# One table part of three loads split into DMAs of 123, 3 and 2 rows

## The chip, the cores and the metric

The kernel runs on one core of one Trainium2 chip. The metric is the device time of one launch in microseconds (us), the median of three runs. A profile of one further execution is read beside it.

## The reference

For 1024 sequences of 50 item numbers the kernel looks up embeddings of 128 values, takes running means over time, normalises them over the batch, runs a spiking neuron over the 50 steps, and multiplies the mean spike count of each sequence with the whole embedding table:

```
e = emb_table[r_seq]                       # 1024 x 50 x 128, row 0 of the table counts as zero
uF = cumsum(e, axis=1) / minimum(t, length)
y = (uF - mean) * rsqrt(var + eps) * gamma + beta
v, spike = scan over the 50 steps          # v += (y - v) / 2; spike when v >= 1; v -= spike
scores = spikes.mean(over steps) @ emb_table.T     # 1024 x 100001, float32
```

The scores are 410 MB, and writing them is most of the traffic.

## The kernel before

The first stage gathers the 50 steps' embeddings by indirect DMA on GpSimd and runs the 50 steps. Beside it SP loads the first 40 parts of the table. A part is 1024 table rows (`HALF`), kept as 128 partitions of 8 table rows each, 4 KB a partition; 98 parts make the table, and the last one has only 673 rows.

The second stage makes the scores. It goes through 21 columns of the output, of 2, 3 and then 6 parts (`WIDTHS`; the last 13 columns have 6), and in each through eight blocks of 128 sequences. A block of a 6-part column is 24 matmuls (`product`, L160, each part being a high and a low half and two banks), six evictions out of PSUM, in turn on DVE (L502) and ACT (L504), and one store of 3 MB on SP's queue (`store`, L169). There are three output buffers of that size, so at most three stores are in flight, and an eviction into a buffer waits until the store before it has landed.

A part is made ready for the matmuls by `prepare`: eight transposes on TensorE (`turned`, L136), a copy on ACT (L152) and a subtraction on DVE (L153). `ready()` calls it between the blocks, about one column ahead of its use, in the order of the parts.

The table parts from 40 on are loaded in the second stage by `fetch`, three parts at a time (1.5 MB), in blocks 1 and 4 of a column:

```
            if n in (1, 4) and c >= MIDDLE and to_fetch < parts:
...
                    fetch(r, k, to_fetch, GROUP // 2)
                    to_fetch += GROUP // 2
```

These loads go out on ACT's queue (`engine = nc.sync if q < held else nc.scalar`), each as one DMA of 128 partitions by three parts (L109). The last load is different, since the last part is short: it goes as one row of 512 B (L120) and 84 rows of 4 KB (L125). The buffers are groups of six parts; two groups are used in turn.

The instructions of each engine run in the order in which the program gives them. The waits between engines, and the semaphores that DMAs complete on, are put in by the framework.

Of the kernel before, what the change touches and what calls it, by code (L numbers as in the profile page):

```python
# [20 lines left out]
P = 128  # L21
BN_EPS = 1e-5
V_TH = 1.0
HALF = 1024
KQ = HALF // P
# [8 lines left out]

WIDTHS = 4 * [2] + 4 * [3] + 13 * [6]
NARROW, MIDDLE = 4, 8


@with_exitstack
def rec_kernel(  # L40
# [49 lines left out]
    def size(q):  # L90
        return min(HALF, N - q * HALF)
# [4 lines left out]
    def group(g):  # L96
        at = g if g < AHEAD else AHEAD - 2 + g % 2
        r = rowp.tile([P, GROUP, HALF], F32, tag=f"rows{at}", name=f"rows_{g}")
        for k in range(GROUP):
            rows[g * GROUP + SHIFT + k if g else k + ASIDE * (k >= TWICE)] = r[:, k, :]  # L100
        return r

    def fetch(r, k, q, n):

        engine = nc.sync if q < held else nc.scalar
        n = min(n, parts - q)
        whole = n - (size(q + n - 1) < HALF)
        if whole:
            engine.dma_start(  # L109
                out=r[:, k : k + whole, :],  # L110
                in_=table[q * HALF : (q + whole) * HALF, :].rearrange("(q p k) d -> p q (k d)", p=P, k=KQ),
            )
        if whole < n:
            full, rest = divmod(size(parts - 1), KQ)
            c1 = (parts - 1) * HALF
            r = r[:, k + whole, :]
            if rest:
                at = full - full % 32
                nc.vector.memset(r[at : at + 32, :], 0.0)
                engine.dma_start(  # L120
                    out=r[full : full + 1, : rest * D],
                    in_=table[c1 + full * KQ : N, :].rearrange("(o k) d -> o (k d)", o=1),
                )
            if full:
                engine.dma_start(  # L125
                    out=r[:full, :],
                    in_=table[c1 : c1 + full * KQ, :].rearrange("(p k) d -> p (k d)", k=KQ),
                )
# [43 lines left out]
    with ExitStack() as ph:  # L172
# [16 lines left out]
        nc.sync.dma_start(out=gb[:, 1:2], in_=beta.rearrange("(d o) -> d o", o=1))  # L189
        first = group(0)  # L190
        fetch(first, 0, 0, TWICE)
        spare = asidep.tile([P, ASIDE, HALF], F32, tag="aside", name="spare")
        for k in range(ASIDE):
            rows[TWICE + k] = spare[:, k, :]
        fetch(spare, 0, TWICE, ASIDE)
        fetch(first, TWICE, SHIFT, GROUP - TWICE)
        for g in range(1, AHEAD):
            fetch(group(g), 0, g * GROUP + SHIFT, GROUP)
# [91 lines left out]
        def over(t, v):  # L290

            d = lp.tile([P, B], BF16, tag="d", name=f"d_{t}")
            nc.scalar.activation(d, v, AF.Identity, bias=less)  # L293
            return d
# [7 lines left out]
        whole = slice(0, B)  # L302
# [6 lines left out]
        for t in range(T):  # L309
# [30 lines left out]
            r = sp.tile([P, 1], F32, tag="r", name=f"r_{t}")  # L340
# [14 lines left out]
            q = sp.tile([P, 1], F32, tag="q", name=f"q_{t}")  # L355
# [20 lines left out]
            if not last:  # L376
# [6 lines left out]
                d = over(t, v)  # L383
# [3 lines left out]
                if t in (T - 8, T - 6):  # L387
                    q = (t - T + 8) // 2
                    pair(q)
                    prepare(q, vp.tile([P, HALF], F32, tag="v1", name=f"pt_{q}"))  # L390
                    if q == TWICE - 1:
                        for k in range(TWICE):
                            rows[GROUP + ASIDE + k] = first[:, k, :]
                        nc.sync.dma_start(
                            out=first[:, :TWICE, :],
                            in_=table[(GROUP + ASIDE) * HALF : (GROUP + SHIFT) * HALF, :].rearrange(
                                "(q p k) d -> p q (k d)", p=P, k=KQ
                            ),
# [55 lines left out]
    for c, W in enumerate(WIDTHS):  # L454
# [34 lines left out]
        for n in range(NB):  # L489
# [26 lines left out]
            if n in (1, 4) and c >= MIDDLE and to_fetch < parts:  # L516
                g, k = divmod(to_fetch - SHIFT, GROUP)
                if k or to_split >= (g - 1) * GROUP + SHIFT:
                    if k == 0:
                        r = group(g)  # L520
# [23 lines left out]
```

## Time and profile before

| | |
|---|---|
| median of three runs | 1576.82 us (1576.77 to 1577.33) |
| the profiled execution | 1636.12 us, span 1633.9 us |
| first store of the second stage | 574.0 us |
| PE, DVE, ACT busy | 66%, 58%, 41% of the span |
| SP's DMA queue (q1) | 430.86 MB, 62.7% of sixteen engines' span |
| ACT's DMA queue (q10) | 30.23 MB, 4.6% |
| HBM | 77.69 MB read, 409.60 MB written |

The profile lists groups of instructions by source line, engine and operation with their count, total and mean time, and what the engine waited for before them. A stage's table gives each engine's busy time in a stretch of the span and the share of time in which the sixteen DMA engines were busy. The chain of waits goes back from the last instruction to whatever released it. All times count from the span's start. Besides these views the trace holds a record for every DMA packet (start, duration, queue, size, but not the engine) and for every update of a semaphore.

### The profile page before, as it was taken

To read this page: it belongs to the slowest core of one execution; us is meant where nothing else is said; L and a number is where in the kernel's file an instruction comes from. 1 tells how busy PE (TensorE), PEld (TensorE's weight loads), DVE (VectorE), ACT (ScalarE), POOL (GpSimd) and SP (SyncE) were. 2 spreads that over 40 slices of the span, in tenths; PEclk is the share of its full clock that TensorE was granted. 3 is DMA by queue.
4 is the path that set the end of the run, shared out by engine and by line. 5 is a ranking of instruction groups with operands and counts; after the bars stand their busy time and mean duration, and the time that the engine had idled before them with its cause. 6 is when DMAs were issued, how large, how long until landed. Compare 5 with 4: busy or idle time off the path is not lost.

```text
span 1633.9 us, 12229 instructions
## 1 busy us (share of the span) xinstructions
PE 1085.1 (66%) x4452; PEld 804.9 (49%) x4452; DVE 944.4 (58%) x1125; ACT 667.5 (41%) x697; POOL 382.2 (23%) x406
## 2 busy tenths in 40 slices
PE   4333422342343498898988878888788888888884
PEld 2112211122122266676866666666666666666663
DVE  5666755676575865665755554555555555545552
ACT  2333322333333355455544444444444444444442
POOL 7666666776766500000000000000000000000000
PEclk9999999999999999999999999999999999999998
DMA  9611111111112189999999999999999999999997
GB/s 349 235 49 49 47 45 44 51 47 44 52 45 60 50 352 416 405 422 415 402 431 423 428 431 425 425 421 418 426 429 421 416 416 417 430 425 417 423 420 330
DMA packets 51313, 488.12 MB, mean 299 GB/s; under 512 B 10079, under 2 KB 10336, under 8 KB 30004
## 3 DMA queue, kind: packets, MB, share of 16 engines
q1 hardware_dynamic: 30752, 430.86, 62.7%
q0 software_dynamic: 12800, 26.24, 5.5%
q10 hardware_dynamic: 7700, 30.23, 4.6%
q8 instruction: 35, 0.57, 0.1%
q14 instruction: 26, 0.21, 0.0%
HBM read 77.69 MB, written 409.60 MB: 298 GB/s over the span
## 4 chain that ended last, share of the span: by engine, by line
DMA 49%; DVE 12%; PE 11%; another core or an unknown queue 8%; POOL 7%; ACT 6%; issue 5%; ACTq 0%; DVEq 0%; SPq 0%; POOLq 0%
DMA scores<-o 46%; PE po L160 10%; POOL e L207 7%; ACT o L504 5%; DVE uF L330 2%; DMA e<-in_L_rec_emb_table,idx 2%; DVE bs L331 2%; DVE v L374 2%; DVE negv L297 2%; DVE o L502 1%; DVE count L300 1%; PE pre L321 1%; ACT v L371 1%; PE pre L281 0%
## 5 line engine op out<-in xcount | busy, mean ns | idle before, releaser
L502 DVE TENSOR_SCALAR o<-po 128x1024 f32<-128x1024 f32 x391 | 463.7, 1221 | 345.8 <-DMA scores<-o 314.0
L504 ACT ACTIVATE o<-po 128x1024 f32<-128x1024 f32 (+1 forms) x391 | 388.9, 1018 | 540.9 <-DMA scores<-o 326.2
L207 POOL DMA_INDIRECT e<-in_L_rec_emb_table,idx x400 | 381.5, 954 | 179.7 <-issue 108.2
L160 PE MATMUL po<-pairs,countB 128*128 128x512 f32 (+1 forms) x1120 | 295.9, 410 | 67.6 <-ACT o L504 52.5
L160 PEld LDWEIGHTS po<-pairs,countB 128*128 128x128 f32 x1120 | 212.9, 195 | 131.3 <-ACT o L504 69.9
L281 PE MATMUL pre<-zT,ls 128*128 128x512 f32 x100 | 78.9, 791 | 270.0 <-DVE uF L330 226.9
L160 PE MATMUL po<-pairs,countC 128*128 128x512 f32 (+1 forms) x840 | 228.1, 418 | 43.6 <-ACT o L504 43.4
L160 PEld LDWEIGHTS po<-pairs,countC 128*128 128x128 f32 x840 | 162.7, 200 | 89.2 <-ACT o L504 55.2
L281 PEld LDWEIGHTS pre<-zT,ls 128*128 128x128 f32 x100 | 29.5, 296 | 309.0 <-DVE uF L330 256.3
L321 PE MATMUL pre<-ident,e 128*128 128x128 f32 x400 | 125.9, 436 | 79.4 <-DMA e<-in_L_rec_emb_table,idx 62.8
L330 DVE SCALAR_TENSOR_TENSOR uF<-rlen,pre 128x512 f32<-128x512 f32 x100 | 68.0, 680 | 166.9 <-remote 132.5
L321 PEld LDWEIGHTS pre<-ident,e 128*128 128x128 f32 x400 | 80.4, 209 | 126.1 <-DMA e<-in_L_rec_emb_table,idx 92.9
L153 DVE TENSOR_TENSOR pairs<-pt,pairs 128x1024 fp32r<-128x1024 f32 x70 | 84.6, 1217 | 90.1 <-ACT pairs L152 90.1
L341 ACT ACTIVATE r<-mv,eps 128x1 f32<-128x1 f32 x50 | 14.7, 295 | 281.7 <-DVE mv L337 185.9
L136 PE MATMUL pt<-ident,rows 128*128 128x128 f32 (+1 forms) x768 | 109.8, 290 | 9.9 <-issue 8.2
L136 PEld LDWEIGHTS pt<-ident,rows 128*128 128x128 f32 (+1 forms) x768 | 99.5, 153 | 27.9 <-issue 12.6
L160 PE MATMUL po<-hi,countB 128*128 128x512 f32 x208 | 86.1, 414 | 16.3 <-ACT o L504 11.1
L160 PE MATMUL po<-lo,countB 128*128 128x512 f32 x208 | 83.6, 402 | 0.0
L293 ACT ACTIVATE d<-v,less 128x1024 bf16<-128x1024 f32 x49 | 54.5, 1113 | 63.5 <-DVE v L374 37.6
L152 ACT CAST pairs<-pt 128x1024 fp32r<-128x1024 f32 x70 | 70.5, 1007 | 16.4 <-PE pt L136 16.3
L160 PE MATMUL po<-hi,countC 128*128 128x512 f32 x156 | 66.3, 425 | 15.2 <-ACT o L504 15.2
L160 PE MATMUL po<-pairs,countA 128*128 128x512 f32 x280 | 70.1, 395 | 9.5 <-ACT o L504 9.5
(85 smaller groups left out, 869.2 us busy)
## 6 DMA issues: line engine op xcount, KB each, us to landing
scores<-o SPq DMA_DIRECT2D x96, 3072.0 KB
scores<-o SPq DMA_DIRECT2D x32, 1536.0 KB
scores<-o SPq DMA_DIRECT2D x30, 1024.0 KB
rows<-in_L_rec_emb_table ACTq DMA_DIRECT2D x19, 1536.0 KB
scores<-o SPq DMA_DIRECT2D x8, 2896.5 KB
rows<-in_L_rec_emb_table SPq DMA_DIRECT2D x5, 3072.0 KB
e<-in_L_rec_emb_table,idx POOLq DMA_INDIRECT x400
rows<-in_L_rec_emb_table SPq DMA_DIRECT2D x2, 1024.0 KB
```

The source lines that it names most:

```text
L136: nc.tensor.transpose(pt[:, k0 : k0 + pw], r[:pw, k0 : k0 + D], ident[:pw, :pw])
L152: nc.scalar.copy(vh, vp)
L153: nc.vector.tensor_tensor(vl, vp, vh.bitcast(F32), ALU.subtract)
L160: nc.tensor.matmul(po[:, :kw], lhsT=counts[n], rhs=part[:, k0 : k0 + kw], start=j == 0, stop=j == 1,)
L207: nc.gpsimd.indirect_dma_start(out=es[t][:, n * P : (n + 1) * P], out_offset=None, in_=table, in_offset=bass.IndirectOffsetOnAxis(ap=idx[: ...
L281: nc.tensor.matmul(pre[h], lhsT=l, rhs=zT[:, h * BANK : (h + 1) * BANK], start=t == 0, stop=False, skip_group_check=True,)
L293: nc.scalar.activation(d, v, AF.Identity, bias=less)
L297: nc.vector.scalar_tensor_tensor(negv, d, 0.0, v, ALU.is_ge, ALU.subtract)
L321: nc.tensor.matmul(pre[h][:, k : k + P], lhsT=e[:, h * BANK + k : h * BANK + k + P], rhs=ident, start=False, stop=last, is_transpose=True, ...
L330: nc.vector.scalar_tensor_tensor(uF[:, cs], rlen[:, cs], 1.0 / (t + 1), pre[h], ALU.max, ALU.mult)
L502: nc.vector.tensor_scalar_mul(o[:, h0 : h0 + hw], po[:, :hw], 1.0 / T)
L504: nc.scalar.mul(o[:, h0 : h0 + hw], po[:, :hw], 1.0 / T)
```

## The change

For three of the loads, those whose first part is 43, 61 or 79, the third part (45, 63 and 81) is taken out of the DMA of three parts. It is loaded by three DMAs of 123, 3 and 2 partitions, issued one after the other on the same queue, and then the other two parts follow as one DMA of 128 partitions by two parts. All other loads, the data and the buffers are as before.

```
+LOW = (43, 61, 79)
...
         whole = n - (size(q + n - 1) < HALF)
+        if q in LOW:
+            whole -= 1
+            n = whole
+            one = r[:, k + whole, :]
+            src = table[(q + whole) * HALF : (q + whole + 1) * HALF, :].rearrange("(p k) d -> p (k d)", k=KQ)
+            p0 = 0
+            for pw in (123, 3, 2):
+                engine.dma_start(out=one[p0 : p0 + pw, :], in_=src[p0 : p0 + pw, :])
+                p0 += pw
+            assert p0 == P
         if whole:
             engine.dma_start(
                 out=r[:, k : k + whole, :],
```

## The prediction

> **What bounds the kernel now.** I read the stages first, then who waits for whom, then the chain of waits, and last the raw records of the stores' completions. The stretches of the second stage (columns: length, then busy time of PE, weight load, DVE, ACT, POOL, then granted clock, DMA share, GB/s):
>
> ```profile
> core 0: us, PE busy (x) PEld busy (x) DVE busy (x) ACT busy (x) POOL busy (x), PEclk, DMA share, GB/s
> 870.00:930.00 60.00, 47.44 (x213) 37.26 (x212) 31.76 (x28) 25.55 (x27) 0.00 (x0) 0.97 1.00 428
> 1240.00:1300.00 60.00, 49.71 (x216) 39.52 (x215) 32.29 (x28) 26.20 (x27) 0.00 (x0) 0.91 0.99 413
> ```
>
> DVE and ACT are about half idle, PE has a fifth free, and the sixteen DMA engines have none. The waits of 880 to 1470 us say the same: the evictions wait for a store to give its buffer back.
>
> ```profile
> DVE o L502 <- DMA scores<-o: 186.2, 66, 5.4
> ACT o L504 <- DMA scores<-o: 178.1, 64, 3.7
> ```
>
> In the chain of waits each store stands with some 20 us, because three are always in flight:
>
> ```profile
> 905.91 20.95 DMA scores<-o
> 926.86 0.02 issue
> ...
> 939.53 21.96 DMA scores<-o
> ```
>
> A store counts sixteen completions, one per DMA engine, and the trace records the time of each. For the store issued at 913.79 fifteen land between 929.8 and 931.9 and the sixteenth at 935.1. It is so for every store from 790 us on: one engine, call it the slow one, is 3 to 9 us behind the middle. The packet records show why. A packet starts 3 to 4 ns before its predecessor on the same engine ends, so one engine's packets can be followed: the slow one needs 936 ns on average for a store row of 24 KB, most others 912. It has no gap, and its stores end 7.5 us apart (8.8 while a load runs). So **the slow engine's own packets set the pace**, and the others are ahead until they run out of stores.
>
> **The skill.** The Trainium skill, "DMA: Bandwidth & Descriptors", section "Why a DMA increments its semaphore by 16 and not by 1", says that a DMA from SP or ACT runs on k engines, k the largest number up to 16 that divides the slowest dimension of both sides, on the lowest-numbered ones, the sequencer writing the rest of the count itself. The rows of the last table part bear on it (durations in ns, min/median/max):
>
> ```profile
> L109 ACTq DMA_DIRECT2D rows<-in_L_rec_emb_table x19: 374/375/469, 864.6 to 1469.8; - x19
> L120 ACTq DMA_DIRECT2D rows<-in_L_rec_emb_table x1: 487/487/487, 1512.4 to 1512.4; - x1
> L125 ACTq DMA_DIRECT2D rows<-in_L_rec_emb_table x1: 808/808/808, 1512.9 to 1512.9; - x1
> ```
>
> L109's loads of 128 rows land with sixteen completions. L125's of 84 rows shows fourteen, between 10.7 and 11.8 us, and one update at 1.0 us, the sequencer's; L120's single row shows one at 5.5 us. The rule holds here and the forecast goes by it: 123 = 3 x 41 and 3 rows run on engines 0 to 2, 2 rows on engines 0 and 1.
>
> The same page, section "Latency and other measured facts", says that engines 7 and 15 are usually the slow ones. The trace can't number the slow engine, but it excludes some: its chain contains packets of the 84-row load (five of six are found), so it is among the first fourteen; and L120's 512 B packet, which must be engine 0's, sits in a chain of 912 ns packets that completes the store of 1511.89 at 1523.7, where the slow one lands at 1531.5. I take engines 0 to 2 to be ordinary ones.
>
> **The change part by part.** It touches the loads issued at 904.87, 1107.27 and 1309.05 (first parts 43, 61, 79).
>
> *Removed.* Each of engines 3 to 15 has 16 load packets instead of 24. A 4 KB packet takes 159 ns less the 4 of overlap, so the slow engine is spared 8 x 0.155 = 1.24 us a load, 3.7 in three.
>
> *Added on engines 0 to 2.* 41 + 1 + 1 packets (engine 2 has no row of the last DMA) in place of 8: 35 x 0.155 = 5.4 us a load. These engines are ahead: by 5.0 us at the store issued at 913.79, in the middle of the sixteen, by 6.5 at 1117.35 and 6.4 at 1319.47. The lead grows by 0.23 us a store (936 less 912 ns, eight times, and a little more), so 24 stores between two such loads bring back 5.5.
>
> *Added on ACT.* Three more issues, each 0.4 to 0.8 us by the three rows above: at most 2.2 us, ahead of evictions for which ACT has 2.4 to 4 us of waiting at each store. Nothing; without that cover 2.2 a load.
>
> *Added waits.* SP's and ACT's DMAs take eight completion semaphores in turn, and one that takes a used semaphore waits for its owner first: ahead of the store at 948.61 SP's records have a wait on the semaphore of the load issued at 904.87. A load gets its semaphore two stores before its place in time. The changed load takes four. The first, of the 123 rows, then comes round at the store of 922.42, where the whole turn came round only at 948.61. So SP holds that store, and every one behind it, until 123 rows have landed. Load and store packets alternate on an engine, a pair taking 1.06 us; by the end of the store of 913.79 (930.0 on a middle engine) some 21 load packets are done, the store queue is empty, and the last 20 follow back to back: 930.0 + 20 x 0.155 = 933.1. The store is then issued at 933.2 and reaches the engines 0.84 later (stores on an idle engine land 8.6 us after issue, eight packets take 7.3 and the receipt 0.48): 934.05. The slow engine ends its packets of 913.79's store at 935.14 - 0.48 - 1.24 = 933.4. It idles 0.65 us.
>
> At the other two the lead starts from nothing, since the hold lets all engines begin together: 5.5 us after 24 stores. The hold ends 5.5 - 20 x 0.155 = 2.4 before the old landing, the store reaches the engines 1.5 before it, and the slow engine is free 1.72 before it: 0.2 us of idling each. Sum for ordinary engines 0 to 2: -3.7 + 0.65 + 0.2 + 0.2 = -2.65.
>
> *Instruction fetches.* 16 KB packets of the instruction queue come every 35 us, each on another engine, and put it 1.9 us behind: four of sixteen stood so at 930, five had been hit in each later stretch. If one of the three engines is among them, that load loses 1.9. With four or five of fifteen hit, it is more likely than not in any one load. I take it for one load of the three, since the hits seem to pass from engine to engine and engines 0 to 2 are neighbours: -2.65 + 1.9 = -0.75.
>
> *What is late next.* The two-part DMA comes behind in the ring of engines 0 to 2: 16 packets. Some 6 to 9 go while the store queue is empty, the rest alternate: landed at 947. It is wanted first at 950.94 by the transposes of part 43:
>
> ```profile
> 950.94 0.48 PEld L136 LDWEIGHTS pt<-ident,rows 128*128 128x128 f32 x3
> 951.17 0.38 PE L136 MATMUL pt<-ident,rows 128*128 128x128 f32 x2
> ```
>
> and by the store of 948.61, which has its semaphore. Hidden by 2 to 4 us. Parts 44 and 45 are wanted at 979.8 and 989.5.
>
> The operation that the trace doesn't show is a load on three engines, whose rows go to partitions that other engines serve. Its packet lies between 155 ns (the same size above) and 300 ns (the slowest hundredth of such packets): 0 to 20 x 0.145 = 2.9 us a load. I take 155, since loads at L125 with fourteen engines show nothing else, and keep 2.9 x 3 for the range. Below nothing the cost can't go further than 3.7 us, the packets taken off the slow engine.
>
> **The forecast.** The profiled execution took 1636.12 us, span 1633.9 and 2.2 around it; it becomes 1635.4. The runs' median is 59 us lower; [...]I carry the -0.75 over: 1576.1. A measurement tells some 0.2%, 3.2 us, from no change, so this is no change; its own range is 1574.2 (no load hit) to 1579.9 (all three hit).
>
> **Rivals.**
> 1. *No hold, late transposes (slower).* If the semaphores fall so that no store is held, the stores keep alternating with the loads. Then 59 load packets and seven stores from 904.5 on end at 904.5 + 7 x 7.27 + 59 x 0.155 = 964.6, landed at 965. PE stands at part 43's transposes from 951 on; four products (0.93 each), their evictions and the transposes bring the next store to 965 + 6.2 = 971.2, on the engines at 972. The slow engine is free at 967.1. Loss 4.9 - 1.24 = 3.7 a load, 11 in all: 1588. It decides once the two-part DMA lands over 2 us behind 960. For it: the ring's order. Against it: the wait seen at 948.61.
> 2. *The slow engine exists only under the profiler (slower).* Then engines 0 to 2 have no lead: the hold ends 3.1 behind the others' store, the next starts 0.94 later and the 0.48 of the receipt counts too; the relief is paid back within that: 4.5 us lost a load, 13.6 in all: 1590.4. For it: the profiled run is 59 us longer. Against it: the first stage has 127 us of stalls under "another core or an unknown queue" that can account for that.
> 3. *The slow engine is 1 or 2 (slower).* It pays 5.4 a load and the hold on top, 7 each: 1598. Against: two of thirteen numbers, and the page's 7.
> 4. *The full relief (faster).* No idling, -3.7: 1573.1. It needs the three engines further ahead than the middle.
>
> **How the numbers follow.** No change or nearly (first case) 0.40, of which 0.04 below -3.2; rival 4 another 0.18; rival 1 0.12; rival 2 0.18; rival 3 0.05; costlier packets or fetches 0.07. Faster by over 0.2%: 0.18 + 0.04 = 0.22. Within: 0.40 - 0.04 = 0.36. Slower: the rest, 0.42. The range 1572.9 to 1590.5 leaves out rival 3 and a third of rival 2 above, together 0.11, and 0.07 below. Cases of both signs hold most of the chance; the likeliest one's range stands above.
>
> **What would show it.** In the changed profile: the loads of 43, 61 and 79 as four issues each; 123 rows with three completions near 28 us after issue; SP waiting some 11 us ahead of the third store after them; the early completions of the next store bunched with the slow one's; the slow engine's stores 8 packets shorter over those loads. PE idle for over 10 us at part 43's transposes would show rival 1, a gap of 4 us or more on the slow engine rivals 2 or 3. A time over 1580 or under 1573 would say that the lead of engines 0 to 2 was misjudged.

## The result, and the profile after

The changed kernel takes 1578.95 us in the median of 14 runs (1577.70 to 1582.37), the kernel before 1576.81 us (1576.05 to 1577.59) beside it: 2.1 us more, ratio 1.0016, 95% interval 1.0009 to 1.0024. The forecast was 1576.1, 0.75 us less than before, in a range of 1574.2 to 1579.9. The result lies in that range, but where no change or a small gain was forecast it is a small loss, and its interval excludes no change. The six of the 14 runs with a mean granted TensorE clock of 0.81 took 1577.70 to 1578.63 us, the eight at 0.94 to 0.96 took 1578.94 to 1582.37.

The profiled run of the changed kernel (clock 0.955) is one of its longest, 1581.87 us with a span of 1579.7. Its first stage is 59 us shorter than in the profile of before (the first store goes out at 514.9 us instead of 574.0), so the spans can't be compared. I compare the second stage: the last 105 stores, from the landing of the first to that of the last. It took 848.00 us before and 853.05 after, **5.05 us more** in this pair of profiles. A time of before less some 60 us is the same place in the profile after.

The stretches that answer to those of the prediction (811 to 871 and 1180 to 1240 us), with three short ones around the first changed load:

```profile
core 0: us, PE busy (x) PEld busy (x) DVE busy (x) ACT busy (x) POOL busy (x), PEclk, DMA share, GB/s
811.00:871.00 60.00, 48.43 (x219) 37.54 (x218) 32.30 (x28) 26.00 (x28) 0.00 (x0) 0.97 1.01 430
860.00:868.00 8.00, 6.41 (x32) 5.00 (x31) 3.83 (x4) 2.96 (x4) 0.00 (x0) 1.00 1.00 424
869.00:878.00 9.00, 7.87 (x39) 6.25 (x38) 5.98 (x6) 4.40 (x5) 0.00 (x0) 1.00 0.90 285
880.00:890.00 10.00, 3.11 (x14) 2.21 (x12) 1.22 (x1) 0.52 (x1) 0.00 (x0) 0.91 0.97 412
1180.00:1240.00 60.00, 46.77 (x215) 36.81 (x214) 32.09 (x28) 25.83 (x27) 0.00 (x0) 0.97 1.01 428
```

Over the longer stretches the DMA engines are full, as before, and move 428 to 430 GB/s (428 and 413 before). Between 869 and 878 us they are still 0.90 busy, but they move 285 GB/s: here the stores stand still. The evictions' waits for stores between 821 and 1411 us are fewer and longer, since a held store holds up its buffer (longest 10.1 and 11.3 us; 5.4 and 3.7 before):

```profile
DVE o L513 <- DMA scores<-o: 189.1, 61, 10.1
ACT o L515 <- DMA scores<-o: 187.9, 60, 11.3
```

The chain of waits around the first changed load. Where the chain of before had a store at each step, it now has the load:

```profile
823.51 19.19 DMA scores<-o
...
846.04 32.04 DMA rows<-in_L_rec_emb_table
878.08 0.02 issue
878.10 0.03 SPq L180
...
878.59 20.76 DMA scores<-o
```

SP stands behind the 123 rows that ACT issued at 846.04 us, and issues three stores one after the other from 878.15 on. It does so at each of the three loads, 71.2 us in all, the longest 24.6 (total, times, longest in the waits of SP's DMA queue, which had no such line before):

```profile
SPq L180 <- DMA rows<-in_L_rec_emb_table: 71.2, 3, 24.6
```

The loads themselves, in the rows of the tile (L116 has the DMAs of 123, 3 and 2 rows, L120 the loads as before and the two-part DMAs, L131 and L136 the short last part):

```profile
L120 ACTq DMA_DIRECT2D rows<-in_L_rec_emb_table x19: 374/375/1186, 805.8 to 1418.2; - x19
L116 ACTq DMA_DIRECT2D rows<-in_L_rec_emb_table x9: 270/1053/1257, 846.0 to 1255.6; - x9
L131 ACTq DMA_DIRECT2D rows<-in_L_rec_emb_table x1: 253/253/253, 1460.1 to 1460.1; - x1
L136 ACTq DMA_DIRECT2D rows<-in_L_rec_emb_table x1: 1039/1039/1039, 1460.4 to 1460.4; - x1
```

The transposes of part 43, which need the two-part DMA, start at 897.77 with no wait noted behind them:

```profile
897.77 1.03 PEld L147 LDWEIGHTS pt<-ident,rows 128*128 128x128 f32 x8
898.00 1.04 PE L147 MATMUL pt<-ident,rows 128*128 128x128 f32 x8
```

The records of the completions, worked out from the trace (us after issue; the gap runs from the end of the last engine's packets of the store before the hold, its landing less 0.48, to the held store's arrival on the engines, its issue plus 0.84):

```
load of   123 rows, 3 completions   two-part DMA: 13 engines, other 3   next load: 13 engines, other 3   gap
43        31.4 31.6 32.0            20.8-21.4     31.6-32.2              7.3-8.4    24.2-27.5           4.2
61        32.3 32.4 34.0            20.3-22.3     32.5-33.9              7.4-7.7    18.5-27.0           5.3
79        31.1 31.8 33.7            20.1-22.9     31.8-33.6              6.7-7.4    14.9-26.7           5.3
```

And the held store of 878.15 itself lands 8.6 to 9.3 us after issue on thirteen engines, 12.4 to 12.5 on three. How late the changed kernel is at the same store (the landing of the whole store after minus before, in us, from the first of the 105 on):

```
store        19     20     23     33     43     44     48     58     67     68     72     82     92    104
after     -0.72  +6.10  +4.22  +1.37  +0.80  +8.70  +6.34  +4.74  +3.58 +11.44  +9.10  +7.58  +5.33  +5.05
                  held                         held                         held
```

Each hold throws the kernel back by 7 to 8 us, of which some 2 come back with the next load's packets, which the gap has already taken in; then it gains 0.1 to 0.3 us a store, and from store 94 on nothing more.

Who is last in between can be read from the sixteen completions of each store. The slow engine is told from the others by its pace: with no load under way it loses some 0.2 us a store on them. The same lateness (against the whole store's landing before) for it and for the three latest of the other fifteen engines:

```
store   slow engine   latest three of the other fifteen
 22       +0.1         +3.7  +3.9  +4.2
 33       -0.1         +0.7  +0.9  +1.4
 43       not told apart; the four latest are -1.0 -0.7 -0.5 +0.8
 48       +2.1         +5.1  +5.3  +6.3
 67       not told apart; the four latest are +0.9 +1.7 +1.7 +3.6
 72       +4.9         +7.4  +7.5  +9.1
 94       +5.0         +2.6  +2.7  +4.9
104       +5.05        +1.2  +1.3  +4.1
```

The other twelve are at -0.9 to -0.6 at store 22. So three engines come out of the first hold far behind all the others. Until store 93 the last engine is not the slow one; then it is again, 5.0 us late. The slow engine itself lost next to nothing by the first load, 2 us by the second and nearly 3 by the third.

### The profile page after: what moved, and what is told of

The parts are those of the page before. It is cut to its first block, busy times and chain, and to the rows that moved or that the text cites. A ratio compares the mean times of both kernels' runs of the same rounds, so it can differ in the third digit from the quotient of the medians.

```text
span 1579.7 us, 12244 instructions
## 1 busy us (share of the span) xinstructions
PE 1111.3 (70%) x4452; PEld 785.6 (50%) x4452; DVE 945.9 (60%) x1125; ACT 667.3 (42%) x697; POOL 381.0 (24%) x406
## 4 chain that ended last, share of the span: by engine, by line
DMA 53%; POOL 18%; PE 12%; issue 8%; ACT 5%; DVE 2%; ACTq 0%; SPq 0%; DVEq 0%; POOLq 0%
DMA scores<-o 43%; POOL e L218 18%; PE po L171 11%; DMA e<-in_L_rec_emb_table,idx 6%; ACT o L515 4%; DMA rows<-in_L_rec_emb_table 4%; DVE o L513 1%; PE pt L147 0%; ACT pairs L163 0%; PE pre L332 0%; DMA idx<-in_r_seq 0%; DVE pairs L164 0%; DVE negv L308 0%; DVE bs L342 0%; DVE uF L341 0%
## 5 line engine op out<-in xcount | busy, mean ns | idle before, releaser
L332 PE MATMUL pre<-ident,e 128*128 128x128 f32 x400 | 179.6, 463 | 230.0 <-DMA e<-in_L_rec_emb_table,idx 229.8
L171 PE MATMUL po<-pairs,countB 128*128 128x512 f32 (+1 forms) x1120 | 289.0, 403 | 64.6 <-ACT o L515 51.7
L171 PEld LDWEIGHTS po<-pairs,countB 128*128 128x128 f32 x1120 | 207.7, 191 | 126.8 <-ACT o L515 68.3
L332 PEld LDWEIGHTS pre<-ident,e 128*128 128x128 f32 x400 | 73.5, 184 | 339.3 <-DMA e<-in_L_rec_emb_table,idx 338.3
L147 PE MATMUL pt<-ident,rows 128*128 128x128 f32 (+1 forms) x768 | 104.6, 281 | 10.3 <-issue 4.9
L147 PEld LDWEIGHTS pt<-ident,rows 128*128 128x128 f32 (+1 forms) x768 | 93.5, 146 | 27.0 <-issue 10.3
L382 ACT ACTIVATE v<-uF,hgb,a 128x1024 f32<-128x1024 f32 x49 | 59.2, 1208 | 30.6 <-DVE a L378 30.5
```

The lines of the kernel that those rows point to most:

```text
L147: nc.tensor.transpose(pt[:, k0 : k0 + pw], r[:pw, k0 : k0 + D], ident[:pw, :pw])
L171: nc.tensor.matmul(po[:, :kw], lhsT=counts[n], rhs=part[:, k0 : k0 + kw], start=j == 0, stop=j == 1,)
L332: nc.tensor.matmul(pre[h][:, k : k + P], lhsT=e[:, h * BANK + k : h * BANK + k + P], rhs=ident, start=False, stop=last, is_transpose=True, ...
L382: nc.scalar.activation(vt, uF[:, cs], AF.Identity, bias=hgb[:, 1:2], scale=a)
```

## The experiments

A, the theory these numbers suggest: **engines 0 to 2 get more than their lead**. A load puts 35 packets more on each of them (5.4 us by count) and the hold makes the last of these packets dear (the expectations take 2.3 us more a load; the count made further on gives 1 to 2). They come out of the hold with a backlog that the others don't have, and set the pace until the slow engine is the last again. Its rivals: the nine additional DMAs and their semaphores cost by themselves; holding the stores costs by itself; a changed load has a fixed price, whatever lies between it and the next. Each expectation explains its letters. On the chip of the first four runs the first stage of every kernel, before's too, took some 60 us longer, so times are compared by ratio and second stages in us. A second stage is that of one profile, and those of f1, f2 and g2 were taken at a clock of 0.81, the others at 0.945 or above.

```
kernel             ratio to before  95% interval        second stage, us   against 848.00
the change         1.0016           1.0009 to 1.0024    853.05             +5.05
e1_even            0.9991           0.9981 to 1.0001    848.63             +0.63
e2_119_7_2         1.0022           1.0012 to 1.0031    852.92             +4.92
e3_123_5           0.9990           0.9979 to 1.0002    846.81             -1.19
e4_late_next       1.0013           0.9998 to 1.0028    851.24             +3.24
f1_one_load        (one run)        -                   848.23             +0.23
f2_close           1.0053           1.0037 to 1.0068    853.86             +5.86
f3_hold_balanced   1.0002           0.9993 to 1.0010    848.46             +0.46
f4_51_64_13        1.0025           1.0015 to 1.0034    849.97             +1.97
g1_five_51         1.0004           0.9996 to 1.0012    847.94             -0.06
g2_last            1.0007           0.9999 to 1.0015    849.49             +1.49
```

**The count of DMAs (e1_even).**

```diff
-            for pw in (123, 3, 2):
+            for pw in (48, 48, 32):
```

> The third part comes in DMAs of 48, 48 and 32 rows, so that each runs on all sixteen engines: same issues, same turn of semaphores, no imbalance. Theory A (the cost is the store that is held until the first of the four DMAs has landed): 48 rows are 3 packets an engine, landed some 7 us after issue, before the store with its semaphore is due; no cost, 1576.8 (0.5 either way). Theory B (the cost is that engines 0 to 2 carry 35 packets more and become the slowest, whatever is held): also 1576.8. Theory C (the cost is the nine more issues on ACT): 1579.

All three sizes divide by sixteen, so each DMA runs on all sixteen engines. The nine additional issues, four semaphores a load and the order of the parts are those of the change. The first DMA lands 8.1 to 9.2 us after issue, SP's waits have no line for the loads, and the second stage is 0.63 us longer, the ratio 0.9991. What costs is not that there are more DMAs.

**Other engines (e2_119_7_2).**

```diff
-            for pw in (123, 3, 2):
+            for pw in (119, 7, 2):
```

> 119, 7 and 2 rows: engines 0 to 6 with 17 or 18 packets instead of 8, engines 7 to 15 none. A: the 119 rows land about 21 us after issue, the store is held some 3 us with two stores still queued, so no engine idles; if the slow engine is 7 or higher it is spared 8 packets a load, 1573.1; if it is one of 3 to 6 it carries 10 or 11 more, 5.1 us in all, 1581 to 1582. B: engines 0 to 6 are given 1.7 us a load, which their lead covers: 1573 too. C: 1579.

The DMAs of 119 and of 7 rows show seven completions each. Engines 3 to 6 then have 17 + 1 + 16 = 34 packets instead of 24. SP waits half as long as in the change:

```profile
SPq L180 <- DMA rows<-in_L_rec_emb_table: 36.1, 3, 12.8
```

Yet the second stage grows by 4.92 us, in three steps of 1.4 to 1.8. Ten packets of 0.155 us in three loads are 4.65. So the slow engine is one of those that this split loads and the change doesn't, engines 3 to 6, and pays for what it is given packet by packet. In the change it was spared eight a load.

**One DMA fewer (e3_123_5), and the next load out of the gap (e4_late_next).**

```diff
-            for pw in (123, 3, 2):
+            for pw in (123, 5):
```

> 123 and 5 rows: one issue less, so the semaphore of the 123 rows comes round one store later; engines 0 to 2 carry as much as in the change. A: the held store is one that is due 9 us later, when the 123 rows have nearly landed; the slow engine does not idle, and it is spared 8 packets a load: 1573 to 1576. B: as the change, 1579. C: 1578.3, six issues of nine.

```diff
-            if n in (1, 4) and c >= MIDDLE and to_fetch < parts:
+            if n in (1, 6 if to_fetch - GROUP // 2 in LOW else 4) and c >= MIDDLE and to_fetch < parts:
```

> The change as it is, but the load that follows each of the three is issued in block 6 of its column instead of block 4. It then gives up its place in the turn of semaphores ahead of the held store, so the store with the first semaphore is one later, as with 123 and 5 rows, and no other load's packets compete with the last ones of the 123 rows. A: no idling, 1573 to 1576. B: engines 0 to 2 still carry as much: 1579. C: 1579.

With three semaphores in place of four (e3) the 123 rows' comes round one store later. One more store is then under way to cover their packets, which land 37.0 to 39.4 us after issue. The gap falls to 0.8, 2.3 and 2.3 us and the loss is gone: -1.19 us, ratio 0.9990, with an interval (to 1.0002) that lies below the change's. Engines 0 to 2 have the same work but for a packet. So the loss hangs on where the hold falls.

In e4 the late next load also moves the hold one store on, and the gaps are those of e3 (0.7, 2.4, 2.7), but the next load isn't there. I had expected a gain, since its packets crowd the 123 rows; instead the second stage is 3.24 us longer, 4.4 more than e3 (the intervals of the two ratios overlap by a little). The two stretches of each kernel show both halves of the matter (first one before the gap, then the gap; e3, then e4):

```profile
925.00:933.00 8.00, 5.89 (x23) 4.64 (x23) 3.51 (x3) 3.29 (x4) 0.00 (x0) 0.79 0.99 424
935.00:943.00 8.00, 7.93 (x39) 6.28 (x37) 4.81 (x4) 3.99 (x4) 0.00 (x0) 1.00 0.92 313
```

```profile
921.00:929.00 8.00, 5.78 (x20) 4.30 (x19) 4.63 (x4) 1.98 (x3) 0.00 (x0) 0.81 0.98 419
931.00:939.00 8.00, 8.00 (x41) 6.63 (x40) 5.79 (x5) 4.48 (x5) 0.00 (x0) 1.00 0.60 247
```

Without the next load the engines are 0.60 busy in the gap, with it 0.92. In e4 all 62 load packets of the gap take 159 ns. In the change (872 to 878 us) 326 load packets take 252 ns on average, a fifth of them 159; in e3 (341 packets, 210 ns) it is half. So the next load does make the packets dear, but what it gets done in the gap is worth more: the slow engine's account in e4 is 5.7 us of gaps in which it did nothing, less 3.7 of relief, +2.0 of the +3.24; the rest isn't accounted for. A had the next load on the wrong side; from here on the account counts only what engines 0 to 2 owe at the hold's end.

**Spacing (f1_one_load, f2_close).**

```diff
-LOW = (43, 61, 79)
+LOW = (79,)                # f1_one_load
+LOW = (79, 85, 91)         # f2_close
```

> Only the load that begins with part 79 is split into 123, 3 and 2 rows; those of 43 and 61 are as before. The figure compared is the second stage, from the landing of its first store to that of its last, against before's. A (engines 0 to 2 get 7.7 us more work at such a load, 5.4 by count and 2.3 because the last packets are dear, and the slow engine's pace gives 0.21 to 0.23 us a store back): they begin 5.5 to 6.5 ahead, fall about 2 behind and have 36 stores to make it good, so the end is again the slow engine's: 5.3 of gap - 3.7 of the next load's packets done in it - 1.24 = +0.4, at most 1 us either way. B (each such load costs its 1.7 us, whatever comes after): +1.7.

> Three loads split as in the change, but those of 79, 85 and 91, with 8 stores between them instead of 24. A (engines 0 to 2 need the stores between to make good 7.7 us a load): 3 x 7.7 - 5.5 of lead - 16 x 0.22 between = 14 behind after the third, 22 stores to the end give back 4.8: second stage +9 us, ratio 1.0055. B (a fixed 1.7 a load): +5, as the change itself in its profile, ratio 1.002 to 1.003.

One load: 1.47 us late at store 68, 0.16 at store 72, 0.23 at the end, which is where it was before the load (0.20). It leaves no lasting price. A's number came out, but not by A's sum: no gap opened on the last engine (-0.5 us), since the 123 rows landed 27.2 us after issue, just as the next load was issued. This is one profile, of a load that finds the three engines further ahead than that of 43 does. Three loads 8 stores apart: ratio 1.0053 where A had said 1.0055 and a fixed price 1.002 to 1.003. The lateness in f2, store by store:

```
store        64     68     72     76     80     84     88     92     96    104
f2_close  +0.03  -1.18  -1.09  +5.03  +3.26 +10.33  +8.49  +7.13  +6.34  +5.86
                  held          held         held
```

The first split load costs nothing (its gap is below zero on the last engine and the 123 rows land at 25.1 to 25.3 us: no load had burdened engines 0 to 2 until then, and the middle of the sixteen lands some 7 us ahead of the last there, against 5 at the load of 43). The second and the third, which find no lead, cost 6 and 7. The third in the chain of waits, a hold of 33.53 us:

```profile
1386.75 33.53 DMA rows<-in_L_rec_emb_table
...
1420.35 12.53 DMA scores<-o
```

The same DMAs of the same sizes cost from nothing to 7 us, by the stores that lie before them. The runs without the profiler say the same: three of f2 took 1583.81 to 1585.30 us, some 8 more than before's 1576.62, where the change, with the same three splits 24 stores apart, costs 2. So what the stores between them bring back isn't a thing of the profiler. A's 9 us lies above the profile's 5.86.

**A hold alone (f3_hold_balanced).**

```diff
+LOW = (43, 61, 79)
...
+        if q in LOW:
+            src = table[q * HALF : (q + n) * HALF, :].rearrange("(q p k) d -> p q (k d)", p=P, k=KQ)
+            engine.dma_start(out=r[:112, k : k + n, :], in_=src[:112, :, :])
+            for j in range(n):
+                engine.dma_start(out=r[112:, k + j, :], in_=src[112:, j, :])
+            whole = n = 0
```

> The loads of 43, 61 and 79 come as one DMA of 112 rows of all three parts, then three of 16 rows, one a part: four semaphores as in the change, but every engine has its 24 packets. The first lands about 25 us after issue, so the third store is held about 16 us by it, in all some 45 to 50. A (a hold costs only where some engines still owe packets at its end): second stage within 1 us of before, ratio 1.000. D (holding the stores is what costs, since the queue runs empty on the ordinary engines): 1.5 to 2 us a load, +5, ratio 1.003.

```profile
SPq L176 <- DMA rows<-in_L_rec_emb_table: 46.1, 3, 16.5
```

SP is held for 46.1 us, as A reckoned (45 to 50), and no gap appears: the 112 rows land 20.5 to 26.0 us after issue, while the stores under way still cover them. The second stage grows by 0.46 us, the ratio is 1.0002. A hold of the stores of 16 us costs nothing when the load ends with the stores on all engines.

**The order (g2_last).** The two-part DMA first, then 3, 2 and 123 rows:

```diff
+        if whole:
+            engine.dma_start(
...
-            for pw in (123, 3, 2):
+            for pw in (3, 2, 123):
```

> The change's three loads with the same rows, sizes and count of DMAs, but the two-part DMA is issued first, then 3, 2 and 123 rows: the semaphore of the 123 rows comes round three stores later, some 32 us after issue instead of 8, and the stores issued until then cover the packets of engines 0 to 2. A (the dear packets and the backlog of the early hold are what exceeds the lead): engines 0 to 2 lose 5.4 to 6 us a load against 5 in hand and 5.5 regained, so the second stage within -1 to +2 us of before, ratio 0.9995 to 1.001. B (35 packets more on three engines cost the same in whatever order): as the change, +5 in its profile, ratio 1.0016.

```profile
SPq L182 <- DMA rows<-in_L_rec_emb_table: 96.7, 7, 20.8
```

Same sizes, same count, and SP is held for longer in all (96.7 us; 71.2 in the change). The 123 rows now hold a store that is due four places later and land 56.7 to 61.8 us after issue. The gaps shrink to -0.9, 1.6 and 1.6 us, the second stage is 1.49 us longer (A: -1 to +2; the change +5.05), the ratio 1.0007. In this pair of profiles the place of the wait decides 3.6 of the change's 5 us. The runs show it less clearly: the intervals of the two ratios overlap, and the two profiles differ in clock (0.810 and 0.955).

**Smaller shares (f4_51_64_13, g1_five_51).**

```diff
-LOW = (43, 61, 79)
+LOW = (43, 49, 55, 61, 67, 73, 79, 85, 91)      # f4; g1: (43, 55, 67, 79, 91)
...
-            for pw in (123, 3, 2):
+            for pw in (51, 64, 13):
```

> Nine loads (every second one from 43 to 91) with the third part as 51, 64 and 13 rows: engines 0 to 2 have 17 + 4 + 1 + 16 = 38 packets instead of 24, engines 3 to 12 have 21, 13 to 15 have 20. A: 51 rows land before the store that waits for them is due by much (22 packets, some 20 us, held 10 and made good like the held stores before), and engines 0 to 2 lose 14 x 0.155 = 2.2 a load where 8 stores bring back 1.8 and 5 are in hand: the slow engine, spared 3 packets, sets the end: 9 x 3 x 0.155 = -4.2, ratio 0.997. B (a price a load, by the packets): 9 x 1.7 x 14 / 35 = +6, ratio 1.004. D (any held store costs 1.5): +13, ratio 1.008.

> As the nine loads of 51, 64 and 13 rows, but five of them (43, 55, 67, 79, 91), 16 stores apart. A: engines 0 to 2 lose 14 x 0.155 = 2.2 us a load, 10.9 in five, and have 5 in hand and regain 0.22 a store over 64 stores between the loads: they never become the last. The slow engine is spared 3 packets a load: 5 x 3 x 0.155 = -2.3 us in the second stage, ratio 0.9985, if the nine loads failed because the lead of engines 0 to 2 was used up. If they failed because each load's stores are held twice (18 waits there), a fixed 1 us each: +2.5, ratio 1.0015.

These were to be the faster version: engines 0 to 2 take 14 packets more, the slow engine three fewer. Both missed, and their profiles are the fastest of their runs (1577.99 us against a median of 1580.29, 1575.67 against 1578.13). f4 is 1.16 us ahead of before at store 44, then falls back as engines 0 to 2 run late: the three-part loads behind the split ones land on them 41 us after issue instead of 28, and stores wait for those too, at every second split load:

```profile
SPq L180 <- DMA rows<-in_L_rec_emb_table: 167.1, 18, 16.1
```

g1 is 1.66 us ahead at store 60 and 0.06 at the end, its next loads landing on the three engines at 31 to 45 us. Its ratio, 1.0004, lies between the two cases named. So the packet count alone overrates what the three engines can take; what else they lose there I haven't measured. No split tried is faster than before by more than the measurement can tell.

## Why the prediction was right or wrong

- *The bound, and the count of engines.* Right. 123 rows show three completions, 3 rows three, 2 rows two, 119 and 7 rows seven. This is the rule of the Trainium skill that the prediction named, and it holds in every DMA tried. After a hold the stores land 7.32 us apart, the ordinary engines' pace, until the slow one is last again.
- *Engines 0 to 2 are ordinary.* Right: e2 puts the slow engine among 3 to 6. The Trainium skill, "DMA: Bandwidth & Descriptors", section "Latency and other measured facts", has 7 and 15 as the usual slow ones, and its guess at the cause is tied to DMAs that GpSimd issues. Here SP and ACT issue, and the measurement decides (+4.92 us for ten packets more on engines 3 to 6).
- *The issues on ACT cost nothing.* Right (e1).
- *The hold.* Right in place and cause: the third store after the load is held by the semaphore of the 123 rows, at all three loads.
- *"At the other two the lead starts from nothing, since the hold lets all engines begin together: 5.5 us after 24 stores."* **This is the step that failed.** When the 123 rows are in, engines 0 to 2 still have the 16 packets of the two-part DMA and the 24 of the next load to do. The others have done the former and most of the latter. The three land the held store 3.1 to 3.9 us after the others; at store 22 they are 3.6 to 4.1 us behind even the slow engine. The 24 stores that were to bring a lead of 5.5 us make this good and little more: at store 43 the four latest engines, the slow one among them, land within 1.8 us. So the second and third holds end late for the slow engine too. Its gap there is the table's 5.3 and what it stood ahead of the last engine, 6.6 to 7.1 and 7.2 to 8.0 us; the next load's 24 packets fill 3.7 (0.155 each, as if alternating with stores), and 1.24 are spared. That leaves +1.7 to +2.2 and +2.2 to +3.0 us where the forecast has 0.2 - 1.24 = -1.0 for each; the completions show 2 and nearly 3. Together with the first load's 0.1 this is the +5.05. f2, with 8 stores between, shows the step at its worst.
- *The hold's length: "the last 20 follow back to back: 930.0 + 20 x 0.155 = 933.1".* Mis-sized. From the end of a middle engine's packets of the store before (872.76 - 0.48 = 872.3) to the end of the 123 rows' (878.08 - 0.48 = 877.6) it took 5.3 us. The load packets of that stretch take 0.255 on average, because the next load is issued in the middle of the hold (at 871.70) and all sixteen engines then read at once. So the rows landed 31.1 to 34.0 us after issue, not near 28. At the other two the three engines were the last of the store before and needed 4.0 and 3.9 us more, at 0.234 and 0.212 a packet. Against 0.155 that is 2.1, 1.3 and 1.0 us. The prediction had the bound (0 to 2.9 us a load, from 300 ns; by the records the slowest hundredth begins at 269) and took its lower end. How much of the backlog of engines 0 to 2 comes from the dear packets, and how much from their count, isn't separated. The 2.3 for every load in the expectations was too much, which may be why f2 came out below the 9 us.
- *The idling of 0.65, 0.2 and 0.2 us.* It was 4.2 - 3.7 = 0.5, and some 3 and 4 us. That the first came out near the forecast is luck: a gap over six times as long was filled by a load that the prediction had not seen at all.
- *The two-part DMA hidden.* Right: it landed on the last engine at 848.71 + 32.2 = 880.9, and the transposes at 897.77 didn't wait for it.
- *An instruction fetch, +1.9 for one load.* Not tried. The unbalanced kernels vary more from run to run (the change by 4.7 us in 14 runs, before by 1.5), and fetches that fall on the three engines may be why; that is argued only. The granted clock goes with it: the change's runs at 0.81 are the shorter ones, and before's are too, by 0.7 to 0.9 us, on the chips of the f and g runs; the cause isn't known. So it stays open why the change's profile shows +5.05 and its median +2.1, and the account above is that of the profile.
- *The rivals.* 1 (no hold, late transposes) fell: there was a hold and no stall on PE. 2 (no slow engine outside the profiler) asked for +13.6 us and no cheaper order; +2.1 and e3's 0.9990, at nearly the same packet count, speak against it. 3 (slow engine 1 or 2) fell with e2. 4 (full relief) didn't come; e3, with seven or eight packets fewer on the slow engine, is as near as the runs of three loads came: -1.19 us of 3 x 7 x 0.155 = 3.3 or more. A time over 1580 was named as the sign that the lead was misjudged; it didn't come, and the lead was misjudged all the same. A gap of 4 us on the slow engine was named as the sign of rival 2 or 3; it came (4.2 at the first load, more at the others) without either.

## What to carry to other kernels

A DMA whose rows don't divide by sixteen can put its bytes on a few engines, and its price then depends on how far those engines are ahead: from nothing to 7 us here for the same 123 rows. Ask which later instruction takes the same completion semaphore, and what each engine still owes when that wait ends; a wait that ended level on all engines was free, one that left three behind was not. Look for every other transfer issued within the wait, and take a packet's duration from such a mix.

## What the runs showed of the hardware that was not expected

A load packet of 4 KB takes 159 ns while stores alternate with it or three engines load alone (all 62 packets of e4's gap), and 252 ns on average, nineteen in twenty under 352, when all sixteen engines read at once with the stores held (872 to 878 us of the change): 285 GB/s in a stretch in which the engines are 0.90 busy, against 424 just before at 1.00. The engines' busy share hardly shows that.
